# Two hand-written step lists for the rounds that drain a software pipeline over 64 graphs

## The chip, the core and the metric

The kernel runs on one core of one Trainium2 chip. A core has five instruction queues that matter here: PE (TensorE, matmuls and transposes), DVE (VectorE), ACT (ScalarE), POOL (GpSimd) and SP (which issues DMAs). The metric is the device time of one execution in microseconds (us). Three runs of the kernel before gave 3460.62, 3468.68 and 3473.94 us, so the median is 3468.68 us. The profile shown below is of one further execution.

## The reference

The input is 64 graphs of 256 nodes with 256 features each, and a 256x256 adjacency matrix per graph. Four layers follow each other. Each one is a graph layer, a residual and a layer normalisation over the features:

```python
def reference(x, adj, ...):
    # layer 0: a recurrence over the 256 nodes, in order (a gated cell per node)
    x = _layernorm(x + _L0_gnn_ref(x, adj, ...))
    # layer 1: normalised adjacency times a linear map
    #   relu((adj * d^-1/2 * d^-1/2) @ (x @ W.T + b))
    x = _layernorm(x + _L1_gnn_ref(x, adj, ...))
    # layer 2: one attention head, masked by adj, with relu on q, k, v and the output
    #   att = softmax(scores * mask - NEG * (1 - mask)); relu((att @ v) @ Wo + bo)
    x = _layernorm(x + _L2_gnn_ref(x, adj, ...))
    # layer 3: eight heads of 32 features, masked where adj is 0
    #   attn = softmax(where(adj > 0, q @ k.T / sqrt(32), NEG)); (attn @ v) @ Wo + bo
    x = _layernorm(x + _L3_gnn_ref(x, adj, ...))
    return x
```

Layers 1 to 3 treat every graph by itself.

## The kernel before

The program has two stages. `_recurrence` does layer 0 for all graphs at once, node after node. `_layers` then does layers 1 to 3, graph after graph, everything in fp32. If a flag that `_layers` computes at its end says so, `_layer_3` repeats layer 3 in a slower form.

`_layers` is a software pipeline. A `Graph` object has one method for each step of a graph's work. The methods that the change moves are these. `xT(l)` transposes the graph's features on PE and ACT copies the result out of PSUM. `qk2`, `v2`, `w2` and `s2` are the matmul products of layer 2 (each is `product`, the matmuls of line 999), with ACT or DVE taking the result. `masks` prepares layer 2's mask on POOL (line 1100). `s2` also finds the row maxima on DVE (lines 1127 and 1013), `exp2` is ACT's exponential (line 1020), `pT2` the transpose of the weights, and `f2` the last product of layer 2 with DVE's bias and residual (lines 1147 and 1151). `norm_a(l)` computes mean and variance on DVE and the power -1/2 on POOL (lines 951 to 955), and `norm_b(l)` a shift on DVE (line 961) and the scaling on ACT (line 963).

Of layer 3, `qk3(s)` are the two projections. `bias_3` stores the features by a DMA and adds a bias on POOL. `s3(hc)` does the scores of four heads: PE writes them to the PSUM tiles `sc0` to `sc3` (line 1183), DVE adds the mask four times (line 1192), ACT takes four exponentials (line 1193), and POOL adds the halves four times (line 1195). `v3` is the value product. `o3` multiplies weights and values of all eight heads and their row sums (lines 1209 and 1218), and writes them into the PSUM tiles `sc0` and `sc1`. `d3(hc)` divides on DVE: a reciprocal, a product, and a check value (lines 1232 to 1234), each reading `sc0` or `sc1`. `f3` is the output product and the residual (line 1241), and `store` is the output DMA (line 1244).

There is one buffer of each of `sc0` to `sc3`. So the scores of one half (`s3.1`) cannot be written before DVE has read those of the other (`s3.0`), and no scores can be written over the outputs of `o3` before `d3` has read them. The other products share four PSUM tiles in rotation.

The order of all instructions is written out by hand (`manual_schedule`). A list of steps, `ROUND` (lines 1248 to 1256), is gone through once in every round. A step is named by a letter and a method. The letter says which graph it works on: in round t, L is graph t+1, A is t, B is t-1, C is t-2 and E is t-3. Each method appends its instructions to the queues of the engines that it uses, so the position of a step in the list is its position in every one of those queues. Steps whose graph does not exist are left out:

```python
for step in ROUND:
    who, name, *args = step.split(".")
    b = t - "LABCE".index(who) + 1
    if 0 <= b < B:
        getattr(graphs[b], name)(*map(int, args))
```

Graph 63 is the last. Its layer 1 (A) is in round 63. In round 64 the steps B of graph 63, C of graph 62 and E of graph 61 remain. In round 65, C of graph 63 and E of graph 62 remain, and in round 66 only E of graph 63.

Of the kernel before, what the change touches and what calls it, by code (L numbers as in the profile page):

```python
# [913 lines left out]
def _layers(tc, ident, Hd, Yd, x, adj, weights, out):  # L914
# [10 lines left out]
    B, N, D = x.shape  # L925
# [5 lines left out]
    with ExitStack() as ctx:  # L931
# [92 lines left out]
        class Graph:  # L1024
# [223 lines left out]
        ROUND = """  # L1248
# [5 lines left out]
            B.pT2 E.norm_b.3 E.store A.norm_b.1 C.s3.1 B.f2  # L1254
            L.adT B.norm_a.2
        """.split()
        graphs = [Graph(b) for b in range(B)]
        graphs[0].load()
        for t in range(-1, B + 3):
            if 0 <= t + 2 < B:  # L1260
                graphs[t + 2].load()
            for step in ROUND:
                who, name, *args = step.split(".")
                b = t - "LABCE".index(who) + 1
                if 0 <= b < B:
                    getattr(graphs[b], name)(*map(int, args))
# [144 lines left out]
def kernel(ctx: ExitStack, tc: tile.TileContext, ins, out):  # L1411
# [25 lines left out]
    )  # L1437
    Yd = dram.tile([B, P, 2, D], F32, name="Yd")
    found = _layers(tc, ident, Hd, Yd, x, adj, weights, out)
    with tc.If(found > 0):  # L1440
        _layer_3(tc, ident, Yd, adj, l3, out)
# [36 lines left out]
```

## Time and profile before

| what | value |
|---|---|
| median of three runs | 3468.68 us |
| the profiled execution, its own time | 3465.43 us |
| span of the profiled execution, first to last instruction | 3463.7 us |
| PE busy over the span | 3228.6 us (93%) |
| DVE, ACT, POOL busy | 72%, 54%, 54% |
| rounds 64 to 66 in that execution | about 3394 to 3463.7 us |
| PE busy in those 69.7 us | 51.47 us |

Times in what follows are microseconds from the span's start. In a timeline row the first two numbers are start and length, then come the engine, the line, the operation, the result and its inputs, and the count; in brackets stand the idle time before it and what ended that. PE is the matmul, PEld the weight load that runs ahead of it. In rows by windows, the count of instructions stands in brackets behind each busy time, and the column behind POOL is the granted clock of PE as a share of full speed.

### The profile page before, as it was taken

What the parts mean: (1) busy time and instruction counts of PE and PEld (TensorE: products, weight loads), DVE (VectorE), ACT (ScalarE), POOL (GpSimd) and SP (SyncE); (2) the same over time, 40 slices, a digit from 0 to 9 for tenths busy, and PEclk for the clock granted to TensorE, in tenths of its full rate; (3) what the DMA queues carried; (4) which work ended last, traced back from release to release, by engine and by line L of the source; (5) the groups of instructions that cost most, each with busy time, mean ns of one, the idle gap of its engine ahead of it and who ended that gap; (6) DMA issues with size and microseconds to landing.
All of it is one profiled execution on the core that took longest, in us unless ns stands there. A gap on an engine that the chain in (4) does not pass through costs nothing.

```text
span 3463.7 us, 80374 instructions
## 1 busy us (share of the span) xinstructions
PE 3228.6 (93%) x29350; PEld 2320.4 (67%) x29350; DVE 2502.0 (72%) x7061; ACT 1883.4 (54%) x5010; POOL 1873.9 (54%) x2181
## 2 busy tenths in 40 slices
PE   5699999999889898887999999999999999999997
PEld 4555555555555555556888888888888888888885
DVE  3366767766666777754888888888888888888875
ACT  0255545444444454444666666666666666666664
POOL 2366677766566777743444444444444444444443
PEclk8999999999999999997999999999999999999999
DMA  9756576687787575321111111111111111111100
GB/s 301 221 153 143 161 173 154 160 187 187 188 208 168 143 175 145 97 64 54 47 47 47 47 47 46 47 47 46 47 47 47 47 47 47 47 47 47 47 28 19
DMA packets 389348, 347.89 MB, mean 100 GB/s; under 512 B 107356, under 2 KB 355304, under 8 KB 383720
## 3 DMA queue, kind: packets, MB, share of 16 engines
q1 hardware_dynamic: 371256, 325.82, 35.0%
q10 hardware_dynamic: 17696, 16.91, 1.5%
q8 instruction: 235, 3.85, 0.5%
q14 instruction: 161, 1.32, 0.1%
HBM read 224.01 MB, written 99.61 MB: 93 GB/s over the span
## 4 chain that ended last, share of the span: by engine, by line
PE 73%; DVE 7%; DMA 7%; POOL 5%; issue 3%; ACT 2%; SPq 2%; ACTq 0%; DVEq 0%; POOLq 0%
PE mm L999 13%; PE rc L607 5%; PE s L1183 4%; PE rc L599 4%; PE mm_2f L999 4%; PE mm_3v L999 3%; PE mm_t L999 3%; PE mm_3f L999 3%; PE mm_2v L999 3%; PE mm_g L999 3%; PE mm_2s L999 3%; DVE ACC L632 3%; PE o L1218 3%; PE mm_2w L999 3%; PE late L523 3%
## 5 line engine op out<-in xcount | busy, mean ns | idle before, releaser
L632 DVE SCALAR_TENSOR_TENSOR ACC<-keep,S,ACC 128x128 f32<-128x128 f32 x1712 | 503.8, 344 | 186.6 <-ACT hs L650 170.7
L1195 POOL TENSOR_TENSOR p3s<-p 128x256 f32<-128x256 f32 x512 | 387.0, 787 | 366.6 <-ACT p L1193 366.2
L999 PE MATMUL mm<-xT,weights 128*128 128x256 f32 x2048 | 481.9, 383 | 2.9 <-ACT xT L1081 2.9
L999 PEld LDWEIGHTS mm<-xT,weights 128*128 128x128 f32 x2048 | 384.8, 190 | 79.5 <-issue 25.5
L1192 DVE TENSOR_TENSOR p<-s,neg 128x512 f32<-128x512 f32 x512 | 317.5, 682 | 114.5 <-PE s L1183 114.5
L669 POOL TENSOR_TENSOR ACC<-ACC,far 128x384 f32<-128x384 f32 (+1 forms) x313 | 372.3, 1189 | 24.5
L599 PE MATMUL rc<-WxT,xqT 128*64 128x256 f32 x2048 | 326.6, 397 | 4.0 <-ACT rc L840 1.2
L665 POOL TENSOR_TENSOR far<-hs,S 128x384 f32<-128x384 f32 (+1 forms) x313 | 304.3, 972 | 4.7
L963 ACT ACTIVATE y<-y,shift,rstd 128x256 f32<-128x256 f32 x512 | 273.4, 599 | 48.6 <-DVE shift L961 44.7
L806 POOL TENSOR_TENSOR ready<-ACC,dinv 128x128 f32<-128x128 f32 x255 | 101.9, 400 | 364.3 <-DVE ACC L632 363.8
L1193 ACT ACTIVATE p<-p 128x512 f32<-128x512 f32 x512 | 295.0, 628 | 2.1 <-DVE p L1192 1.6
L1106 ACT ACTIVATE qk<-mm,weights 128x256 f32<-128x256 f32 x256 | 107.5, 471 | 268.0 <-PE mm L999 268.0
L1095 POOL TENSOR_TENSOR y<-y,g 128x512 f32<-128x512 f32 x64 | 81.0, 1265 | 267.4 <-issue 267.4
L1232 DVE RECIPROCAL rT<-o 128x256 f32<-128x256 f32 x128 | 223.7, 1748 | 0.2 <-PE o L1209 0.2
L955 POOL TENSOR_TENSOR rstd<-rstd,mhalf 128x2 f32<-128x2 f32 x256 | 173.6, 696 | 84.2 <-DVE rstd L954 82.4
L951 DVE BATCH_NORM_STATS2 st<-y 128x6 f32<-128x256 f32 x512 | 208.8, 408 | 13.4 <-POOL y L1095 12.6
L616 ACT COPY xpT<-xpT_ps 128x128 f32<-128x128 f32 x256 | 68.4, 267 | 265.6 <-PE xpT_ps L614 265.6
L607 PE MATMUL rc<-WhT,xpT 128*64 128x128 f32 x2048 | 170.5, 288 | 28.2 <-ACT xpT L616 28.0
L1060 POOL TENSOR_TENSOR dis<-dis,mhalf 128x2 f32<-128x2 f32 x64 | 44.8, 700 | 277.0 <-DVE dis L1059 252.1
L607 PEld LDWEIGHTS rc<-WhT,xpT 128*64 128x64 f32 x2048 | 107.9, 137 | 118.4 <-ACT xpT L616 84.0
L212 PE MATMUL xp<-xX,xA 128*128 128x256 f32 x384 | 109.4, 423 | 66.3 <-POOL xA L685 39.5
L1158 ACT ACTIVATE qk<-mm,weights 128x256 f32<-128x256 f32 x256 | 107.5, 471 | 115.9 <-PE mm L999 115.9
(162 smaller groups left out, 7485.1 us busy)
## 6 DMA issues: line engine op xcount, KB each, us to landing
xX<-in_x_dram ACTq DMA_DIRECT2D x16, 1024.0 KB
Us<-xu SPq DMA_DIRECT2D x64, 256.0 KB
xq<-in_x_dram SPq DMA_DIRECT2D x64, 256.0 KB
ACC<-Us SPq DMA_DIRECT2D x32, 512.0 KB
Es<-eu SPq DMA_DIRECT2D x64, 256.0 KB
early_sb<-Es SPq DMA_DIRECT2D x32, 512.0 KB
xin<-in_x_dram SPq DMA_DIRECT2D x64, 256.0 KB
ad<-in_adj_dram SPq DMA_DIRECT2D x64, 256.0 KB
```

What stands on the lines that cost most here:

```text
L599: nc.tensor.matmul(G[o * B:(o + 1) * B], xqT[a, i // 2][:, i % 2, kc, h * B:(h + 1) * B], WxT[:, kc, o, gates], start=False, stop=False, s ...
L607: nc.tensor.matmul(G[o * B:(o + 1) * B], hT[:, kc * B:(kc + 1) * B], WhT[:, kc, o, g], start=False, stop=(kc == 1), skip_group_check=True,)
L632: nc.vector.scalar_tensor_tensor(acc[:, 0, :], keep[:, j % 2, :], s, acc[:, 0, :], ALU.mult, ALU.add)
L665: nc.gpsimd.tensor_mul(tmp[:, 0:count, :], hs.unsqueeze(1).to_broadcast(shape), s.unsqueeze(2).to_broadcast(shape),)
L669: nc.gpsimd.tensor_add(acc, acc, tmp[:, 0:count, :])
L951: nc.vector.bn_stats(st, y[:, c, :])
L963: nc.scalar.activation(y[:, c, :], y[:, c, :], AF.Identity, bias=shift[:, c:c + 1], scale=rstd[:, c:c + 1],)
L999: nc.tensor.matmul(pm[:, c, :], lhsT[:, k, c * P:(c + 1) * P], rhs[:, k, :], start=(k == 0), stop=(k == 1),)
L1192: nc.vector.tensor_add(p, s_ps[i], self.neg3)
L1193: nc.scalar.activation(p, p, AF.Exp, scale=ISQ)
L1195: nc.gpsimd.tensor_add(both, p[:, 0, :], p[:, 1, :])
L1232: nc.vector.reciprocal(rT, o_ps[:, 1, :])
```

## The change

A dictionary `LAST` holds two step lists. Round 64 (t - B = 0) and round 65 (t - B = 1) take theirs from it, and all other rounds keep `ROUND`. Both lists hold exactly the steps that `ROUND` leaves for these rounds. No instruction is added, removed or resized; only the order in the queues differs.

```diff
+
+        LAST = {
+            0: """
+                B.xT.2 B.masks B.qk2.0 B.qk2.1 E.o3 E.d3.0 B.s2 B.exp2 C.norm_b.2 E.d3.1
+                B.v2 C.xT.3 C.bias_3 B.w2 C.qk3.0 B.pT2 B.f2 B.norm_a.2
+                C.qk3.1 E.f3 C.s3.0 C.v3 E.norm_a.3 E.norm_b.3 E.store C.s3.1
+            """.split(),
+            1: """
+                C.norm_b.2 C.xT.3 C.qk3.0 C.qk3.1 E.o3 E.d3.0 E.d3.1 C.bias_3 C.s3.0 C.v3
+                E.f3 C.s3.1 E.norm_a.3 E.norm_b.3 E.store
+            """.split(),
+        }
         graphs = [Graph(b) for b in range(B)]
         graphs[0].load()
         for t in range(-1, B + 3):
             if 0 <= t + 2 < B:
                 graphs[t + 2].load()
-            for step in ROUND:
+            for step in LAST.get(t - B, ROUND):
                 who, name, *args = step.split(".")
                 b = t - "LABCE".index(who) + 1
                 if 0 <= b < B:
```

For comparison, `ROUND` without the steps whose graph does not exist reads, in round 64:

```
B.xT.2 E.o3 E.d3.0 B.qk2.0 C.norm_b.2 E.d3.1 B.qk2.1 B.v2 B.masks E.f3 C.xT.3 C.bias_3
C.qk3.0 C.qk3.1 E.norm_a.3 B.s2 B.exp2 C.s3.0 C.v3 B.w2 B.pT2 E.norm_b.3 E.store C.s3.1 B.f2 B.norm_a.2
```

and in round 65:

```
E.o3 E.d3.0 C.norm_b.2 E.d3.1 E.f3 C.xT.3 C.bias_3 C.qk3.0 C.qk3.1 E.norm_a.3 C.s3.0 C.v3
E.norm_b.3 E.store C.s3.1
```

## The prediction

> **What bounds the kernel now.** I first read the page for the whole: PE is busy 93% of the span and is 73% of the chain that ended last. The change touches only rounds 64 to 66, so I read those by windows.
>
> ```profile
> 3394.00:3421.00 27.00, 25.94 (x175) 19.83 (x174) 17.80 (x41) 15.28 (x35) 9.37 (x13) 1.00 0.06 21
> 3421.00:3444.00 23.00, 17.32 (x118) 11.12 (x116) 14.81 (x31) 8.15 (x17) 8.54 (x11) 0.85 0.06 24
> 3444.00:3463.70 19.70, 8.22 (x58) 4.42 (x58) 9.54 (x21) 3.64 (x7) 3.62 (x6) 0.76 0.08 29
> ```
>
> Round 64 is still full on PE (25.94 of 27.00). Rounds 65 and 66 are not: no engine is full there, and the time is the dependency chain of graph 63. The whole tail is 69.7 us, 2% of the span, so only a few us are to be had. Next the timeline of the tail, graph 63's chain alone:
>
> ```profile
> 3396.53 0.58 ACT L1081 COPY xT<-tr_x 128x512 f32<-128x512 f32 x1
> ...
> 3410.70 1.70 PEld L999 LDWEIGHTS mm_2s<-qk,qk 128*128 128x128 f32 x8
> ...
> 3419.36 1.59 PEld L999 LDWEIGHTS mm_2f<-w,pT 128*128 128x128 f32 x8 [0.73 <-ACT pT L1140]
> ...
> 3427.73 1.09 ACT L963 ACTIVATE y<-y,shift,rstd 128x256 f32<-128x256 f32 x2 [5.36 <-DVE shift L961]
> ...
> 3433.70 0.59 ACT L1081 COPY xT<-tr_x 128x512 f32<-128x512 f32 x1 [4.88 <-PE tr_x L989]
> ...
> 3438.62 0.84 PEld L1183 LDWEIGHTS s<-qk,qk 32*128 32x128 f32 x16 [0.97 <-ACT qk L1158]
> ...
> 3439.85 2.48 DVE L1192 TENSOR_TENSOR p<-s,neg 128x512 f32<-128x512 f32 x4 [4.76 <-PE s L1183]
> ...
> 3443.21 2.48 DVE L1192 TENSOR_TENSOR p<-s,neg 128x512 f32<-128x512 f32 x4 [0.42 <-PE s L1183]
> ...
> 3445.71 1.76 DVE L1232 RECIPROCAL rT<-o 128x256 f32<-128x256 f32 x1
> ...
> 3450.89 2.21 PEld L999 LDWEIGHTS mm_3f<-weights,oT 128*128 128x128 f32 x6 [2.08 <-DVE oT L1233]
> ```
>
> They are, in order: layer 2's transposed features, scores and last product, layer 2's normalisation, layer 3's transposed features, the first scores, both halves of the mask additions, the first reciprocal of d3.0, and the last product. After it come 12.8 us that the change does not touch. Two waits look removable: s2 stands 14 us behind xT, and y63 waits until 3427.73 and then for graph 62's f3 on PE.
>
> The clock of PE matters where it idles:
>
> ```profile
> 3424.00:3427.00 3.00, 0.70 (x5) 0.14 (x2) 2.86 (x7) 0.00 (x0) 0.92 (x2) 0.99 0.03 5
> 3427.00:3430.00 3.00, 1.35 (x3) 0.63 (x3) 2.90 (x7) 1.09 (x2) 0.00 (x0) 0.50 0.09 37
> 3430.00:3433.00 3.00, 3.00 (x8) 2.36 (x9) 0.45 (x3) 0.00 (x0) 0.00 (x0) 0.50 0.13 51
> 3433.00:3436.00 3.00, 2.33 (x12) 1.74 (x11) 1.95 (x6) 0.59 (x1) 1.97 (x2) 0.87 0.00 0
> ```
>
> The granted clock halves after PE fell idle at 3424.9 and is back at about 3433.8. The row at 3450.89 again takes 2.21 for six weight loads where 1.59 does for eight.
>
> [...]an idle stretch of 1.6 us (from 3449.2) also preceded a drop.[...]
>
> **The change part by part.** Nothing is added or removed, so all 69.7 us are a matter of who waits. I rework the tail with the durations of before: product 1.73 on PE and its result 2.03 after its start; four transposes 0.44, result at 0.85; o3 3.0, its sc0 part at 1.70; scores 1.08, result at 1.15; d3 2.67 per half, its oT at 2.27; four additions 2.48; ACT's four exponentials start 0.75 and POOL's four sums end 4.33 to 4.7 after the additions' start.
>
> *Round 64, first half.* xT63 cannot come earlier than 3397.1, since ACT does graph 61's exponentials until 3396.5. Before, o3 of 61 filled PE meanwhile; now PE idles 2.0. Then q, k, o3 and s2: 3397.16+1.73+1.73+0.2+3.0 puts s2 at 3403.9 (before 3410.70, gain 6.8), its result at 3405.9, exp2 done 2.3 later at 3408.2. The moved norm_b.2 of graph 62 stands behind exp2 on ACT: 3409.3. PE has only v2 (to 3407.4) and waits for it, idle another 2.0. Then tr_x62, w2, qk3.0, tr_p: 3409.4+0.9+1.73+1.73+0.44; the copy of pT ends 3415.5 and f2 starts there: gain 3.8.
>
> *Round 64, second half.* Behind f2 now stand qk3.1 and f3 (3.46), so s3.0 of 62 starts at 3421.0 (before 3412.73) and s3.1 at 3424.3 (before 3417.89). DVE's four additions run 3422.15 to 3424.65 and POOL's sums end at 3426.5. norm_a.3 of 61 stands behind those sums on POOL, and DVE waits for its power (0.70) in shift61 until 3427.2. Queued behind that wait are the additions of s3.1 (3427.4 to 3429.9), then shift63; on ACT, y61, four exponentials (to 3431.0), then y63. So y63, whose variance was ready at 3421.9, is done at 3432.1, and tr_x63 starts there: before 3432.17. The gain of 3.8 is used up, and PE has idled 6.6 (from 3425.5).
>
> *Round 65.* tr_x63, xT, q, k at half clock as before, then o3 of 62 and only then d3 of 62. Transposes and copy 1.53+0.64, q and k 3.45, and a cold extra of 1.7 ([...]bounds 0 and 3.4) put o3 at 3439.6. s3.0 of 63 needs sc1, which d3.1 of 62 frees at 3439.6+1.70+5.34=3446.65. Before, it stood behind nothing at 3438.62. PE idles 4 us in this wait, so scores, v3 and f3 start cold: extra 1.95 (bounds 0 and 3.4). The first additions start at 3447.75 (before 3439.85). s3.1 follows s3.0, v3 and f3: 3446.65+1.08+0.3+3.46+0.2+1.95=3453.6, its additions at 3454.8 (before 3443.21: +11.6).
>
> *Round 66.* DVE now has norm_a.3 of 62 and shift62 behind the additions, and shift62 waits for a power on POOL that stands behind graph 63's last four sums: 4.7+0.7+0.25, so the reciprocal comes 5.65 after the additions' start, 3460.45 instead of 3445.71 (there 2.5 after): +14.7. Less 0.25 that DVE waited before the second reciprocal: +14.5.
>
> *Cold clock in round 64.* Two idle stretches of 2.0 lie on the path. Each may cost 1.7 [...]or nothing. I take one: +1.7, bounds 0 and 3.4.
>
> Costed at nothing: masks on POOL stays at 3399.46, behind the same rstd62, and is needed at 3406.6. The Yd stores and bias_3 have tens of us until f3 adds; if a store were late by more than 5 us, POOL's sums would slip with it. Output stores keep their order on SP; that of 62 (256 KB) moves to about 3461, still clear of the last.
>
> Sum: 14.5+1.7 = +16.2. Against the profiled execution, 3465.43+16.2 = 3481.6; on the median, 3468.68+16.2 = 3484.9. The runs spread by 13 us, so I say 3484.
>
> **The rivals.** A measurement of this kernel can tell about 0.5%, or 17.3 us, from no change.
>
> *Clock kept up.* If no new idle stretch costs clock, 1.7+1.95+1.7 go: +10.9, about 3479. The six weight loads at 3450.89 speak against it: idle of 1.6 sufficed.
>
> *Slower by more.* If each of the three cold terms takes its upper bound, 3.4+3.4+3.4 replace 5.35: +21, about 3490.[...] For it: the two 2.0 idles exceed the 1.6 that sufficed.
>
> *The chain does come forward.* f2 is 3.8 earlier, and if that reached the end, the time would be 3464.9. It needs sc1 free by 3438.7, hence o3 of 62 at 3431.6 and tr_x63 at about 3426.5. The order on ACT speaks against that, with y63 behind graph 62's last exponential, and so does d3's 5.34 in front of the scores, which stood beside f3 and xT before.
>
> That the list does not do what it says is excluded: the order is written out, and the instructions stand in it.
>
> **How the numbers follow.** Main case (+13 to +17.3) 0.42; slower by more (+17.3 to +26) 0.38; clock kept up (+5 to +13) 0.14; forward (-6 to +2) 0.06. Spread between runs moves some of the slower case below the bound and some of the main case above it: slower 0.45, same 0.53, faster 0.02. The range leaves out the forward case and the far end: +4.5 to +25, 3473 to 3494.
>
> **What would show it.** In the changed profile: s2 about 7 us and f2 about 4 us earlier; shift61 on DVE waiting for POOL; ACT's y63 behind graph 62's exponentials, tr_x63 near 3432; PE idle some 6 us ahead of it and 4 us ahead of s3.0 of 63, at clock 0.5; the scores of 63 released by DVE's d3.1; the recip of 63 released by shift62. It is wrong if y63 overtakes the exponentials, if o3 of 62 finishes before q and k, or if scores of 63 start before d3.1 ends.

## The result

The changed kernel takes 3480.76 us, the median of 19 runs (3474.81 to 3486.71), against 3468.68 us for 19 runs of the kernel before. The ratio is 1.0036, with a 95% interval from 1.0029 to 1.0044: 12.1 us slower. The forecast was 3484. It lies 3.2 us above the median, and its range of 3473 to 3494 holds it. The loss is inside the 0.5% that was set as the bound for no change, and the interval shows that it is real.

The profiled execution of the changed kernel has a span of 3476.6 us, 12.9 more than before. The tail, from graph 63's first weight load of round 64 to the end of the span, grew from 69.4 (3394.27 to 3463.7) to 82.2 (3394.43 to 3476.6). So nearly the whole difference is in the three rounds at the end.

First the windows of the changed kernel, one for each stage of the tail. The stages end where PE falls idle behind round 64, and where o3 of graph 63 starts.

```profile
3394.40:3424.90 30.50, 26.07 (x174) 19.44 (x173) 18.07 (x43) 13.48 (x30) 8.68 (x12) 1.00 0.05 19
3424.90:3454.70 29.80, 19.43 (x116) 13.31 (x117) 11.97 (x22) 9.55 (x19) 8.17 (x11) 0.71 0.05 18
3454.70:3476.60 21.90, 8.39 (x58) 4.33 (x58) 11.18 (x27) 4.52 (x8) 4.20 (x6) 0.64 0.07 26
```

Before, PE was busy for 25.94 of the 27.0 us of round 64. Now round 64 takes 30.5 us for the same work, with 4.4 us of idle time on PE. The middle stage is the worst: no engine is full, and PE's clock averages 0.71.

Then the timeline of the changed kernel, the rows that answer to those of graph 63's chain before:

```profile
3403.70 1.59 PEld L999 LDWEIGHTS mm_2s<-qk,qk 128*128 128x128 f32 x8 [0.41 <-issue]
...
3414.65 1.59 PEld L999 LDWEIGHTS mm_2f<-w,pT 128*128 128x128 f32 x8 [1.21 <-ACT pT L1140]
...
3426.23 0.16 DVE L961 SCALAR_TENSOR_TENSOR shift<-mv,rstd 128x2 f32<-128x2 f32 x1 [1.27 <-POOL rstd L955]
...
3430.14 0.18 PEld L989 LDWEIGHTS tr_x<-ident,y 128*128 128x128 f32 x1 [5.69 <-ACT y L963]
...
3439.85 1.76 DVE L1232 RECIPROCAL rT<-o 128x256 f32<-128x256 f32 x1 [10.93 <-PE o L1218]
...
3445.27 2.08 PE L1183 MATMUL s<-qk,qk 32*128 32x256 f32 x14 [1.93 <-DVE far L1234]
3446.64 2.67 DVE L1192 TENSOR_TENSOR p<-s,neg 128x512 f32<-128x512 f32 x4 [1.51 <-PE s L1183]
...
3453.89 2.48 DVE L1192 TENSOR_TENSOR p<-s,neg 128x512 f32<-128x512 f32 x4 [0.44 <-PE s L1183]
...
3458.96 0.16 DVE L961 SCALAR_TENSOR_TENSOR shift<-mv,rstd 128x2 f32<-128x2 f32 x1 [0.81 <-POOL rstd L955]
3459.04 1.75 DVE L1232 RECIPROCAL rT<-o 128x256 f32<-128x256 f32 x1
```

Layer 2's scores of graph 63 came 7.0 us earlier and its last product 4.7. The transposes for layer 3 (3430.14, before 3432.17) kept only 2.0 of that, since ACT scaled y63 behind graph 62's exponentials. Then the loss begins. DVE idles 10.93 us until o3 of graph 62, which now stands behind q and k. The scores of 63 wait for DVE's last read of sc1. The final reciprocal waits behind shift62, which waits for POOL.

The chain of waits of the changed kernel shows the same stretch as one path, start and length in us:

```profile
3432.21 6.14 PE mm L999 x16
3438.35 0.57 PE o L1209 x8
3438.92 0.91 PE o L1218 x16
...
3439.85 1.77 DVE rT L1232
...
3442.53 1.68 DVE rT L1232
...
3445.27 2.08 PE s L1183 x14
```

q and k, then o3, then both halves of d3 of graph 62 are now in series, and the scores of graph 63 come after them. In the chain of waits of the kernel before, d3 and q and k were in series too, the other way round:

```profile
3425.04 1.67 DVE rT L1232
...
3427.69 1.68 DVE rT L1232
...
3429.88 2.93 PE mm_3f L999 x6
3432.81 0.87 PE tr_x L989 x4
...
3434.34 3.73 PE mm L999 x16
...
3438.62 1.22 PE s L1183 x15
```

From the start of this series to the scores it was 13.6 us before (3425.04 to 3438.62), and it is 15.1 now (3430.14 to 3445.27). The larger part of the loss up to here is that the series starts 35.7 us into the tail and not 30.8. It now begins with the transposes, which wait for y63. o3 and d3 of graph 62 do not need y63, only POOL's sums of graph 62 (the last ends at 3430.97), but in PE's queue o3 stands behind the transposes, q and k. PE idled 5.3 us in the wait for y63.

### The profile page after: what moved, and what is told of

Read it like the earlier page. It is cut to its first block, busy times and chain, and to the rows that moved or that the text cites. A ratio compares the mean times of both kernels' runs of the same rounds, so it can differ in the third digit from the quotient of the medians.

```text
span 3476.6 us, 80372 instructions
## 1 busy us (share of the span) xinstructions
PE 3236.3 (93%) x29350; PEld 2326.2 (67%) x29350; DVE 2503.4 (72%) x7061; ACT 1884.2 (54%) x5010; POOL 1875.5 (54%) x2181
## 4 chain that ended last, share of the span: by engine, by line
PE 71%; DVE 7%; DMA 7%; POOL 6%; issue 4%; ACT 2%; SPq 2%; ACTq 0%; DVEq 0%; POOLq 0%
PE mm L999 13%; PE rc L607 4%; PE s L1183 4%; PE mm_2f L999 4%; PE mm_3v L999 3%; PE mm_t L999 3%; PE rc L599 3%; PE mm_2s L999 3%; PE mm_g L999 3%; PE mm_3f L999 3%; PE o L1218 3%; PE mm_2v L999 3%; PE mm_2w L999 3%; DVE ACC L632 3%; PE late L523 3%
## 5 line engine op out<-in xcount | busy, mean ns | idle before, releaser
L599 PE MATMUL z_ps<-WxT,xqT 128*64 128x128 f32 x2048 | 170.5, 288 | 0.0
```

The costliest lines, as they stand in the source:

```text
L599: nc.tensor.matmul(G[o * B:(o + 1) * B], xqT[a, i // 2][:, i % 2, kc, h * B:(h + 1) * B], WxT[:, kc, o, gates], start=False, stop=False, s ...
```

## The experiments

Each profile is compared by its tail, as defined above: 69.4 us before, 82.2 changed. Ahead of the tail the kernels are the same, but the profiled executions differ there by up to 14 us (the tail starts between 3387.69 and 3401.59), so the tail tells more than the total. Each tail is that of one execution. Whether the last f3 met the full or the half clock makes about 1 us of it (its six weight loads took 1.16 at a clock of 1.00 in the mended lists, 2.21 at 0.50 in the kernel before). The table also has the time from the tail's start to the last scaling of graph 63 on ACT (line 963), which leaves the final store out.

| kernel | tail | to the last scaling |
|---|---|---|
| before | 69.4 | 62.8 |
| changed | 82.2 | 75.7 |
| list of round 64 alone | 71.2 | 64.6 |
| list of round 65 alone | 79.2 | 72.6 |
| o3 of 62 ahead of xT of 63 | 71.9 | 65.0 |
| normalisation of 62 last | 78.9 | 72.4 |
| PE kept busy | 75.3 | 70.4 |
| two waits of round 64 removed | 79.6 | 72.7 |
| mended lists | 63.2 | 56.4 |
| mended lists, bias ahead | 62.3 | 55.6 |

### Each list alone

```diff
         LAST = {
             0: ...
-            1: ...
         }
```

> Only round 64 takes its own list; round 65 keeps ROUND. Tail = from graph 63's first weight load of tr_x in round 64 to the end of the span: 69.4 us before, 82.2 us changed. Theory (the loss sits in round 65, where the scores of 63 wait for d3.1 of 62, and in round 66 behind shift62): with ROUND's order in round 65, o3 of 62 starts as soon as POOL's sums allow, tr_x63 stands behind f3 of 62 near 3436 instead of 3432, and the tail is 73 (72 to 76). Rival (the loss is made in round 64, by the delay of graph 62): 79 or more.

Measured: tail 71.2, ratio to before 1.0016 (1.0004 to 1.0027) from 11 runs against 18. The rival falls. The tail is 0.8 below the lower end of the theory's 72 to 76. In this profile the clock of PE was full at both f3 of layer 3 that wait for d3 (1.00 in the windows from 3438.00 to 3466.50): six weight loads took 1.16 where they took 2.21 before. Each time that is some 1.0 us. With that clock as before, the tail would be about 73.

```diff
         LAST = {
-            0: ...
             1: ...
         }
```

> Only round 65 takes its own list; round 64 keeps ROUND. Tail 69.4 us before, 82.2 us changed. Theory: tr_x63 starts near 3427, 5 earlier than before, but o3 of 62 stands behind q and k, d3 of 62 holds sc1 until about 3441, and norm_a.3 and shift62 stand ahead of the last reciprocals: tail 77.5 (75 to 80). Rival (the loss is made in round 64): at or under 70.

Measured: tail 79.2, ratio 1.0035 (1.0020 to 1.0049) from 8 runs against 18. The theory holds. The loss sits mainly in round 65's list: 9.8 alone, against 1.8 for round 64's list (nearly 4 with the clock as before), and 12.8 with both. Round 64's list was meant to bring graph 63 forward, and it does so for f2 of 63. But with round 65's list alone tr_x63 starts 32.4 us into the tail (3431.38 in this profile), and with both lists 35.7. So it sets graph 63 back by 3.3 us where layer 3 begins.

### One step back: o3 of graph 62 ahead of xT of graph 63

```diff
-                C.norm_b.2 C.xT.3 C.qk3.0 C.qk3.1 E.o3 E.d3.0 E.d3.1 C.bias_3 C.s3.0 C.v3
+                C.norm_b.2 E.o3 C.xT.3 C.qk3.0 C.qk3.1 E.d3.0 E.d3.1 C.bias_3 C.s3.0 C.v3
```

> The changed kernel with one step of round 65 moved: E.o3 from behind C.qk3.1 to ahead of C.xT.3. DVE's order stays the same. Theory (the wait for sc1 behind o3): o3 of 62 runs in PE's idle time ahead of tr_x63, d3.1 ends about 3434.5, the scores of 63 start near 3438, released by ACT's k and no longer by DVE: tail 75 (73.5 to 77), from 82.2. Rival (the half clock of PE makes the loss): at most 1.5 gained.

Measured, in one execution as for the three kernels after it: tail 71.9. This one step is worth 10.3 of the 12.8 us, more than the theory's 5 to 9, and the rival falls. The timeline of this kernel, whose tail starts at 3400.61:

```profile
3436.16 1.76 DVE L1232 RECIPROCAL rT<-o 128x256 f32<-128x256 f32 x1 [1.05 <-PE o L1218]
...
3437.76 0.42 PEld L989 LDWEIGHTS tr_x<-ident,y 128*128 128x128 f32 x4 [0.41 <-issue]
...
3439.09 3.72 PE L999 MATMUL mm<-xT,weights 128*128 128x256 f32 x16 [0.68 <-ACT xT L1081]
...
3443.38 0.84 PEld L1183 LDWEIGHTS s<-qk,qk 32*128 32x128 f32 x16 [0.97 <-ACT qk L1158]
```

The scores of 63 are released by ACT's k, as the theory said, and no longer by DVE, whose d3.1 ended its reads at 3441.4. Counted from the start of the tail they begin 42.8 us in; in the changed kernel it was 50.8. The 8.0 us come apart in three. The transposes start 1.4 later, since o3 stands ahead of them. From their start to the end of ACT's copy of k, 5.9 replace 9.1, mainly because q and k ran at full clock (3.72 on PE for both at 1.00; 6.14 in the changed kernel, at 0.50 until 3437.14). And the 6.0 from there to the release of sc1 are gone, with another 0.3 because the first scores need only the first half of k. From the scores to the last additions of s3.1, 6.1 replace 8.7. So the move took away the wait, and with it idle time and the half clock that followed. Of the 10.6 gained by then, some 5 are the clock's, an estimate: 2.4 on q and k (6.14 less 3.72) and the 2.6 from the scores on (8.7 less 6.1). The next run parts the two.

### The clock by itself

```diff
+            def warm(self, n):
+                for i in range(n):
+                    pm = product(W3["q"], W3["k"], f"warm_{self.b}_{n}_{i}")
...
-                C.qk3.1 E.f3 C.s3.0 C.v3 E.norm_a.3 E.norm_b.3 E.store C.s3.1
+                C.qk3.1 E.f3 C.s3.0 C.v3 E.norm_a.3 E.norm_b.3 E.store C.s3.1 E.warm.3
...
-                C.norm_b.2 C.xT.3 C.qk3.0 C.qk3.1 E.o3 E.d3.0 E.d3.1 C.bias_3 C.s3.0 C.v3
+                C.norm_b.2 C.xT.3 C.qk3.0 C.qk3.1 E.o3 E.d3.0 E.d3.1 C.bias_3 E.warm.2 C.s3.0 C.v3
```

> The changed kernel with five products more on PE whose results nothing reads: three behind the scores of 62 at the end of round 64, two ahead of the scores of 63, both in PE's idle time (extra work, PE only). Tail 82.2 us changed, 69.4 before. Theory: PE's clock stays full, which takes off 1.9 between tr_x63 and o3 of 62 and 2.2 between the release of sc1 and s3.1 of 63; the scores still wait for d3.1, so the tail is 78 (76.5 to 79.5). Rival (the half clock makes most of the loss): under 74. Rival (the clock costs nothing there, being hidden behind DVE): 82 or more.

Measured: tail 75.3, outside the 76.5 to 79.5 of the theory. To the last scaling the gain is 5.3 (75.7 to 70.4); the other 1.6 us is after it, from the last scaling to the end of the span (4.9, in all other kernels here 6.5 to 6.9), and stays unexplained. First the windows of the changed kernel, then those of this one:

```profile
3427.00:3430.00 3.00, 0.00 (x0) 0.00 (x0) 1.92 (x4) 3.00 (x8) 1.82 (x3) 0.50 0.25 87
...
3433.00:3436.00 3.00, 3.00 (x9) 2.37 (x8) 0.00 (x0) 0.00 (x0) 1.08 (x1) 0.50 0.00 0
...
3444.00:3447.00 3.00, 1.73 (x14) 1.29 (x14) 1.42 (x5) 0.00 (x0) 0.00 (x0) 0.50 0.00 0
3447.00:3450.00 3.00, 3.00 (x9) 2.19 (x7) 2.22 (x4) 2.45 (x4) 1.88 (x3) 0.50 0.00 0
```

```profile
3429.00:3434.00 5.00, 5.00 (x24) 4.16 (x23) 3.69 (x9) 3.31 (x7) 2.91 (x5) 1.00 0.14 52
3434.00:3441.00 7.00, 6.12 (x40) 4.26 (x42) 0.00 (x0) 3.39 (x8) 2.88 (x4) 1.00 0.10 40
3441.00:3447.00 6.00, 6.00 (x55) 4.16 (x46) 5.14 (x8) 0.10 (x1) 0.00 (x0) 1.00 0.00 0
3447.00:3453.00 6.00, 6.00 (x48) 4.45 (x46) 3.17 (x5) 2.90 (x5) 2.79 (x4) 1.00 0.00 0
```

With work in the gaps the clock stays at 1.00 where it had been at 0.50. Counted from the start of the tail, o3 of 62 starts 41.2 us in instead of 43.9 (2.6 gained, 1.9 expected), and s3.1 of 63 52.9 instead of 58.2. So another 2.7 came between these two points (2.2 expected). The half clock costs 5.3 of the changed kernel's tail, which is more than the theory's 4.1, and less than half of the 12.8. Both rivals fall. The wait for d3.1 is still there. What remains against before is 7.6 us to the last scaling. The kernel before had its own half clock for some 7 us (0.50 from 3427.0 to 3433.8), so the order costs somewhat more than this difference.

### The last normalisation of graph 62, and two waits of round 64

```diff
-                E.f3 C.s3.1 E.norm_a.3 E.norm_b.3 E.store
+                E.f3 C.s3.1
+            2: E.o3 E.d3.0 E.d3.1 F.norm_a.3 F.norm_b.3 F.store E.f3 E.norm_a.3 E.norm_b.3 E.store
```

In this diff and in those below the quotes of the lists are left out. F is a new letter, for graph t-4.

> The changed kernel with the last normalisation of graph 62 and its store moved from the end of round 65 to behind d3.1 of 63 in round 66, where DVE and POOL are idle. Theory: the reciprocal of 63 starts 2.5 us after the start of the last four additions instead of 5.15, so the tail is 79.5 (79 to 80.5), from 82.2. Rival (that DVE's wait for POOL is covered by o3's own wait for the sums): no change, 82.

Measured: tail 78.9, 3.3 gained, against the theory's 2.7. The rival falls. The timeline of this kernel:

```profile
3451.74 2.48 DVE L1192 TENSOR_TENSOR p<-s,neg 128x512 f32<-128x512 f32 x4 [0.44 <-PE s L1183]
...
3454.14 1.75 DVE L1232 RECIPROCAL rT<-o 128x256 f32<-128x256 f32 x1
...
3461.52 0.16 DVE L961 SCALAR_TENSOR_TENSOR shift<-mv,rstd 128x2 f32<-128x2 f32 x1 [0.81 <-POOL rstd L955]
3461.60 0.69 DVE L1241 TENSOR_TENSOR y<-y,mm_3f 128x512 f32<-128x512 f32 x1
```

The reciprocal comes 2.4 after the start of the additions, where the changed kernel needed 5.15. That is the gain which was expected. The rest is two things that work against each other. The last f3 ran at full clock (its six weight loads took 1.16), and shift62 at its new place made graph 63's residual (line 1241) wait.

```diff
-                B.xT.2 B.masks B.qk2.0 B.qk2.1 E.o3 E.d3.0 B.s2 B.exp2 C.norm_b.2 E.d3.1
+                B.xT.2 B.masks B.qk2.0 B.qk2.1 C.norm_b.2 E.o3 E.d3.0 B.s2 B.exp2 E.d3.1
...
-                C.qk3.1 E.f3 C.s3.0 C.v3 E.norm_a.3 E.norm_b.3 E.store C.s3.1
+                C.qk3.1 E.f3 C.s3.0 C.v3 C.s3.1
...
-                C.norm_b.2 C.xT.3 C.qk3.0 C.qk3.1 E.o3 E.d3.0 E.d3.1 C.bias_3 C.s3.0 C.v3
+                C.norm_b.2 C.xT.3 C.qk3.0 C.qk3.1 E.o3 E.d3.0 E.d3.1 F.norm_a.3 C.bias_3 C.s3.0 F.norm_b.3 F.store C.v3
```

> The changed kernel with two waits of round 64 taken out by moving steps: norm_b.2 of 62 ahead of o3 and exp2 (so ACT does y62 early and PE does not idle before tr_x62), and the normalisation of 61 and its store into round 65, behind d3.1 of 62 (so DVE does not wait for POOL in shift61 ahead of the additions). Theory: f2 of 63 1.5 us earlier, tr_x63 of round 65 2.8 earlier (33 us after the start of the tail instead of 35.7), the rest in the same order: tail 79.4 (78.5 to 80.5), from 82.2. Rival (these waits are covered by ACT's exponentials): 81.5 or more.

Measured: tail 79.6, within the theory's range. f2 of 63 starts 19.2 us into the tail, 1.0 earlier and not 1.5. The additions of s3.1 of 62 start 3.3 behind those of s3.0 (3413.47, 3416.75), where they started 5.1 behind (3421.19, 3426.31), and tr_x63 comes 32.8 us into the tail. It had been 35.7. The rival falls.

The gains of these four edits (10.3, 5.3, 3.3 and 2.6) do not add up to the 12.8 us, because they overlap: the move of o3, for one, takes away half clock as well.

### Lists that beat both kernels

The runs say what a list for these rounds has to keep. o3 of 62 has to run before q and k of 63, so that DVE's 5.3 us of d3 lie beside them. The normalisations of 61 and 62, in which DVE waits for POOL, have to go where DVE waits for graph 63 anyway. And PE should have work in its gaps. These lists do so, and start round 64 with o3 of 61, as `ROUND` does:

```diff
+            0: B.xT.2 E.o3 E.d3.0 B.masks B.qk2.0 C.norm_b.2 E.d3.1 B.qk2.1 B.v2 B.s2 C.xT.3 C.bias_3
+               B.exp2 B.w2 C.qk3.0 B.pT2 C.qk3.1 B.f2 B.norm_a.2 C.s3.0 C.v3 E.f3 C.s3.1
+            1: C.norm_b.2 E.o3 E.d3.0 C.xT.3 C.qk3.0 C.qk3.1 E.d3.1 F.norm_a.3 F.norm_b.3 F.store
+               C.bias_3 E.f3 C.s3.0 C.v3 C.s3.1
+            2: E.o3 E.d3.0 E.d3.1 F.norm_a.3 E.f3 F.norm_b.3 F.store E.norm_a.3 E.norm_b.3 E.store
```

> Own lists for rounds 64 to 66, with graph 63 still ahead in round 64, but: o3 of 61 first, y62 ahead of exp2, scores of 62 before any normalisation of 61, shift63 and o3 of 62 ahead of q and k of 63, the normalisations of 61 and 62 in rounds 65 and 66 where DVE waits. Theory: d3.1 of 62 is done before ACT has k of 63, so the scores of 63 start near 37 us after the tail's start (44.4 before, 50.8 changed) and the tail is 62.5 (60 to 66): about 7 us or 0.2% faster than before. Rival (new waits on the FIFO queues take it back, as in the changed kernel): 69 or more.

Measured: tail 63.2, ratio to before 0.9984 (0.9974 to 0.9994), with medians of 3462.46 us over 22 runs against 3465.67 over 27. The medians alone would give 0.9991; the ratio uses all runs. The scores of 63 start 37.7 us into the tail, and the clock stays full until the last product is done (1.00 from 3398.90 to 3454.50). Of the theory's 7 us, 6.2 are there in the tail, and the rival falls.

One wait was new. The timeline of the mended lists:

```profile
3436.82 0.37 SPq L1244 DMA_DIRECT2D out_dram<-y  x1
...
3437.24 0.46 SPq L1164 DMA_DIRECT2D Yd<-y  x1
...
3439.82 1.27 POOL L1165 TENSOR_TENSOR y<-y,weights 128x512 f32<-128x512 f32 x1 [4.64 <-ACT p L1193]
...
3441.05 5.54 POOL L1195 TENSOR_TENSOR p3s<-p 128x256 f32<-128x256 f32 x8
```

On SP the store of 63's features (line 1164) stood behind the output store of 61, which waits for 61's normalisation. POOL's bias waits until that DMA has read the features, and POOL's eight sums stand behind the bias. The row of the bias names ACT's exponential as the last releaser, but the bias reads nothing of it. It starts 2.58 after the issue of the store. In the next run it starts 2.59 after it (3430.49, 3433.08), and there the row names the DMA.

```diff
-            1: C.norm_b.2 E.o3 E.d3.0 C.xT.3 C.qk3.0 C.qk3.1 E.d3.1 F.norm_a.3 F.norm_b.3 F.store
-               C.bias_3 E.f3 C.s3.0 C.v3 C.s3.1
+            1: C.norm_b.2 E.o3 E.d3.0 C.xT.3 C.bias_3 C.qk3.0 C.qk3.1 E.d3.1 F.norm_a.3 F.norm_b.3 F.store
+               E.f3 C.s3.0 C.v3 C.s3.1
```

> The mended lists with one step moved: C.bias_3 of round 65 from behind the store of 61 to behind C.xT.3. In the mended lists the DMA of Yd stood on SP behind the store of 61, POOL's bias waited for it until 3439.82, and POOL's sums of 63 and so o3 and the reciprocal of 63 came late: 4.2 us after the start of the last additions instead of 2.5. Theory: the reciprocal comes 2.5 after them again, and the tail from graph 63's first weight load to the end of the span is 61.5 (60.5 to 62.5), from 63.2. Rival (the sums are late for another reason, POOL's own 2.8 us for four): no change.

Measured: tail 62.3, ratio 0.9985 (0.9978 to 0.9992), 3462.04 us over 22 runs against 3466.87 over 27. The reciprocal comes 2.5 after the start of the additions again (3442.54, 3445.04), as the theory has it. Half of the 1.7 was given back, because the last f3 was slower in this profile: its six weight loads took 1.97, where they took 1.16 in the mended lists, and 2.21 at a clock of 0.50 in the kernel before. In time the two mended versions cannot be told apart. Both beat the kernel before by some 0.15%, and the interval of each lies below 1.

## Why the prediction was right

The mechanism held in every step but one, the cold clock of round 64, and the sum was 3.3 us too high: +16.2 was forecast for the profiled execution, +12.9 of span came. That step alone is 1.7 of it. The rest came out near in part by luck: tr_x63 was forecast 2.1 us too late, counted from the start of the tail, and the cold extras of round 65 were 1.65 too small, and these two errors offset each other. By its steps:

| step of the prediction | forecast | profile after |
|---|---|---|
| s2 of 63 | 3403.9 | 3403.70 |
| f2 of 63 | 3415.5 | 3414.65 |
| s3.0 of 62 | 3421.0 | 3420.02 |
| shift61 behind POOL | to 3427.2 | 3426.23 |
| tr_x63 of round 65 | 3432.1 | 3430.14 |
| o3 of 62 | 3439.6 | 3438.28 |
| scores of 63 after sc1 | 3446.65 | 3445.24 |
| first additions of 63 | 3447.75 | 3446.64 |
| last additions of 63 | 3454.8 | 3453.89 |
| reciprocal of 63 | 3460.45 | 3459.04 |

The trace after starts the tail 0.16 later than the one before, so each forecast is that much further off.

**Round 64, first half.** Right, with f2 0.9 too late in the forecast. It let tr_x62 wait until all of y62 was scaled. In the trace the transposes start with the first half, at 3408.67 instead of 3409.4.

**Round 64, second half.** The order of waits was right: shift61 waited 1.27 for POOL, the additions of s3.1 stood behind it, and y63 behind the exponentials. The end of the chain was mis-sized by 2.0. Of these, 1.1 came with the additions of s3.1, which started at 3426.31 and not at 3427.4, as all before them was early. The exponentials ended 3.3 after the start of the additions and not 3.6. And the transposes started with the first half of y63 (3430.14, y63 ends 3430.58), once more. So the gain that reached tr_x63 was 2.0 and not 0.1.

**Round 65.** Right in kind: the scores waited for d3.1 behind o3, and the row names DVE as the releaser. The cold extras were forecast at 1.7 and 1.95, both the author's estimates. The run with PE kept busy measured 2.6 and 2.7, so they were 1.65 too small in the sum.

**Round 66.** Right in size: the reciprocal came 5.15 after the start of the additions (5.65 forecast), and the run that moved the normalisation away brought it to 2.4.

**Cold clock in round 64.** Wrong. 1.7, an estimate again, was forecast for one of two idle stretches of 2.0. The trace has idle stretches of 2.24 and 1.65 there on the weight loads, and the clock stayed at 1.00 through all of round 64. The evidence for that term was one idle stretch of 1.6 ahead of a drop in the kernel before, and here a longer one had none behind it. The last section has the measured times.

**The rivals.** The clock kept up took off 5.35 of cold terms and came to +10.9. The run with PE kept busy gained 5.3 and came to +7.6, both to the last scaling. So that rival had the worth of the clock nearly right in the sum, which is luck: none of it lay in round 64, where it took off 1.7, and all of it in round 65. As a forecast it fails, since the clock did fall in the new idle stretches of round 65. The rival in which the chain comes forward needed sc1 free at 3438.7, which is 44.4 us into the tail. In the changed kernel d3.1 ended its reads 50.7 us in. In the mended lists it ends 34.2 us in, and there the chain does come forward, by 6 us. The slower rival needed drops in round 64, and there were none; in round 65 the extras were 2.6 and 2.7 of its 3.4 each, a bound that was the author's estimate.

## What to carry to other kernels

Moving the longest chain to the front of every queue does not make it run first. It also moves back what the chain needs later: here the o3 and d3 of the graph before, which hold the PSUM tiles that the chain's own scores are written to. Before such a move, follow each single buffer that the chain will take and ask who reads it last, and then look for the step that waits for another engine and stands ahead of the chain in the same queue (here shift61 and shift62 on DVE, which waited 1.27 and 0.81 us for POOL). In a tail where no engine is full, keep the filler in the gaps, since idle time on PE was paid twice here, once as a wait and once as half the clock behind it (5.3 us, by the run with PE kept busy).

## What the runs showed of the hardware

The granted clock of PE is not told by the length of an idle stretch alone. After 2.24 us on the weight loads (3395.1 to 3397.3 in the changed kernel) it stayed at 1.00. In the kernel before it dropped to 0.50 at 3450.82, at the end of a stretch of 2.08 on the weight loads, 1.6 of it idle on the matmuls as well. After PE fell idle at 3424.9 in the changed kernel it dropped at about 3427, two us later. In the run with o3 ahead it dropped to 0.50 within an idle stretch of 2.65, for some 3.4 us. Five products that nothing reads, put into the gaps, held it at 1.00, and that was worth 5.3 us of a tail of 82.

Nor did the busy time just ahead tell it. In the changed kernel the clock dropped at 3426.90, 3443.96 and 3461.03, and in the 3.41 us ahead of each drop PE's matmuls were busy for 1.36, 1.19 and 1.16 us. In the kernel before they were busy for 1.73 of the 3.41 us ahead of the drop at 3450.82. But from 3394.00 to 3397.41 in the changed kernel they were busy for no more than 1.41, and the clock stayed at 1.00. (The ends of matmuls are modelled in the profile, so these times are rough.) The half clock that ended inside the tail lasted 10.24 us (3426.90 to 3437.14) and 6.83 us (3443.96 to 3450.79) in the changed kernel, and 6.83 and 3.41 us in the kernel before. What decides whether an idle stretch costs the clock was not shown.
